# A fused mixture-of-experts layer on one core: the first loads dealt to two queues, and new ranks for the order of the work

## The chip, the cores and the metric

The kernel runs on one core of a Trainium2 chip. A core has a matrix engine (TensorE, PE in the profile, with its weight loads as PEld), three engines for everything else (VectorE, DVE; ScalarE, ACT; GpSimd, POOL) and SyncE (SP), which here only issues transfers. Transfers between the chip's main memory and the core's memory are carried by 16 DMA engines; an instruction on SP, ACT or POOL issues one. Each engine works through its own list of instructions in order and waits on semaphores for the others. The metric is the time of one execution in microseconds (us), as the median of several runs.

## The reference

Sixteen sequences of 256 tokens with 256 features go through a layer of eight experts and one shared expert. Every token goes through every expert, and the outputs are weighted for each sequence:

```python
E, B, S, D, F = (8, 2, 256, 256, 1024)   # B is 16 in the call
h = hidden_states
g = jnp.einsum('bsd,edf->ebsf', h, Wg)
u = jnp.einsum('bsd,edf->ebsf', h, Wu)
expert_outs = jnp.einsum('ebsf,efd->ebsd', jax.nn.silu(g) * u, Wd)
expert_output = jnp.einsum('be,ebsd->bsd', gating_probs, expert_outs)
shared = jnp.einsum('bsf,fd->bsd', jax.nn.silu(h @ Sg) * (h @ Su), Sd)
sg = shared_gate_prob[:, :, None]
return x + (1.0 - sg) * expert_output + sg * shared
```

All values are 32-bit floats. Wg, Wu and Wd are the weights of gate, up and down.

## The kernel before

The work is cut into 72 units, `units` in line 1361: nine experts, two halves of the 1024 hidden features, four groups of four sequences, the group innermost. A unit multiplies the tokens of its group by half an expert's gate and up weights, applies silu and the product, and multiplies by half of the down weights. To save matmuls, four token blocks and four weight blocks are combined (sums and differences in pairs) so that fewer products give all the blocks; this is why there are so many additions on VectorE and GpSimd. PE products carry the names D (the four diagonal pairs), M and X (the six pairs off the diagonal) and dn (the down product). Units 4 to 55 keep sums over experts in another form (`star`, line 640), units 56 to 71 go back to the first form. Unit 0 is plain: it multiplies the raw tokens by the raw weights (lines 814 to 853), since it comes first and the combined forms are not there yet.

Nothing is issued in the order in which it is written. Each piece of work is an `Op` with an engine, an estimated length, a rank, and what it depends on; `load` (line 358), `tt` and `stt` (lines 364 to 374) and `mm` (line 644) make them. `Plan.run` (line 105) then plays through the program once while it is being built: whenever an engine comes free, it takes from what is ready there the piece of the lowest rank. PE's pieces go strictly by rank, in two streams (the up side and dn). What comes out is a fixed list for each engine. The table `RANK` (line 25) holds the numbers that ranks are made of; many of them apply only to some units. `seed`, `sc`, `p` and `st` belong to the units of the star form, `wq` and `wqa` to the units from 56 on, `ph`, `hX`, `hA`, `hD`, `hE`, `hF` and `hG` to the sums of tokens and weights that units 1 to 4 make, `hR` to the sums of group 0's raw tokens, `pa` to a scaling on ScalarE in the pairs of weights (`make_pair`, line 416), `back` to the moments at which buffers return after the star form.

The start runs like this. `make_raw` (line 546) loads the four token blocks of group 0 (256 KB each, called x0 to x3 below, tile `side`), PE transposes each (line 561), ScalarE copies the result to `pq` (line 566). `load_base` (line 383) loads a half of the gate or up weights in two loads of 256 KB, for features 0 to 127 (`u`) and 128 to 255 (`v`), into a tile `wb`; sums are later made in the second part, so `load_raw` (line 443) loads features 128 to 255 of gate and up once more, into a tile of its own. Unit 0 reads `u` of `load_base` as its first half and the tile of `load_raw` as its second. The lines that set the order are these:

```python
        if n == 0:
            make_raw(0, (-14, -6.97), (-20, -18.6))
            load_base(0, e, half, -16, (-19, -16))
            first_raw = load_raw((-18.8, -17.5))
            load_base(1, e, half, -15, (-18, -15))
            make_raw(1, (-5.5, -5.5), (-17, -17))
```

The last pair of each line is the ranks of its loads. On SP the order that follows is: x0; gate's first half; gate's second half (called G2 below); x1; up's first half; up's second half; x2; x3; then gate's and up's `v`; then the tokens of groups 1 and 2. Before all of that GpSimd issues two broadcasts of the routing weights, `p_bc` and `coef` (lines 335 and 339), and PE runs nine products of zeros (line 354) while it has nothing else. The first two columns of gate's product are taken in halves (lines 827 to 843), so that x0 can be used before x1 is there.

Of the kernel before, what the change touches and what calls it, by code (L numbers as in the profile page):

```python
# [22 lines left out]


RANK = {
    "first": 4, "q": 2.85, "dc": 2.45, "acc": 2.55, "g": -5.35, "cp": 1.85, "seed": -0.3, "s": 0.75,
    "lagx": 1.0, "sc": 15.85, "bank": (6.6, 7.1, 8.6, 15.9, 16.4, 16.9, 17.3), "ev": 0.3, "p": 2.3,
    "xc": 0.2, "st": 1.2, "qa": -2.0, "da": -1.25, "ga": -7.25, "pace": 2, "m0": 1.9, "m1": 2.5, "xm":
    0, "w": 16, "mp": 4, "m2": 1.5, "ml": 1.75, "lagw": 1.0, "wp": -0.95, "wq": -0.9, "wqa": -2.25,
    "wdc": 2.2, "ws": 0.5, "wseed": 0.2, "wxc": 0.95, "pa": -4.25, "hd": (), "ph": 7.25, "pd": 1.0,  # L30
    "xh": 5, "hX": 4.5, "hA": 10.5, "hR": 5.0, "hD": -6.5, "hE": 5, "hF": -7.75, "hG": -3.75, "to":
    (-18, -3, -9, -16, -46), "back": (-27, 120, 21, -15, -5, 80, 20),
}


# [29 lines left out]
class Plan:  # L65
# [27 lines left out]
    def add(self, engine, length, rank, emit, deps=(), new=(), uses=(), lag=None, kb=None, port=False):  # L93
        lag = self.HOP if lag is None else lag
        op = Op(engine, length, lag, rank, emit, deps, list(new), list(uses))
        for b in [*op.new, *op.uses]:
            b.users += 1
        op.kb = kb
        op.port = port
        if engine == "PE" and op.new and op.new[0].tag == "dn" or "dn" in [b.tag for b in op.uses]:  # L100
            op.stream = 1 if engine == "PE" else None
        self.ops.append(op)
        return op
# [101 lines left out]
def kernel(  # L205
# [112 lines left out]
    def act(n):  # L318
        return 0.21 + n * 0.000625
# [38 lines left out]
    def load(rank, dst, src, kb, deps=(), new=(), uses=(), late=0, engine="SP"):  # L358
        queue = {"SP": nc.sync, "ACT": nc.scalar}[engine]
        return add(  # L360
            engine, 0.5, rank, lambda: queue.dma_start(dst(), src), deps, new, uses, lag=2.2 + late, kb=kb  # L361
        )

    def tt(engine, rank, o, a, b, op, n, deps, new=(), uses=(), port=True):
        eng, length = (nc.vector, dve(n)) if engine == "DVE" else (nc.gpsimd, pool(n))
        return add(engine, length, rank, lambda: eng.tensor_tensor(o(), a(), b(), op), deps, new, uses, port=port)  # L366
# [9 lines left out]
    def sources(e):  # L376
        return (Wg[e], Wu[e], Wd[e]) if e < E else (Sg, Su, Sd)
# [5 lines left out]
    def load_base(m, e, half, rank, ranks=None):  # L383
        b = Buf("wb", f"wb_{m}_{e}_{half}")
        src = [
            sources(e)[m][ts(part, P), ts(half, 4 * P)].rearrange("p (c q) -> p c q", q=P)
            for part in range(2)
        ] if m < 2 else None
        late = 0 if rank < 0 else 8
        ru, rv = ranks or (rank, rank)  # L390
        if m == 2:
            rows = sources(e)[2][ts(half, 4 * P), :].rearrange("(c p) (k q) -> p c k q", p=P, q=P)
        if m == 2:
            u = v = load(ru, lambda: b.tile, rows, 512, [], [b], late=late)
        else:
            u = load(ru, lambda: b[:, :, 0, :], src[0], 256, [], [b], late=late)
            v = load(rv, lambda: b[:, :, 1, :], src[1], 256, [], [], [b], late=late)
        ops = []
        for i, t in enumerate(POINTS):
            r, x_ = (lambda i=i: b[:, i, 1, :]), (lambda i=i: b[:, i, 0, :])  # L400
            if t == 0:
                op = v
            elif abs(t) == 1:
                op = tt("POOL", rank + 1, r, r, x_, ALU.add if t > 0 else ALU.subtract, P, [u, v], uses=[b])
            elif e == half == 0:
                op = stt(rank + 1, r, x_, float(t), r, ALU.add, P, [u, v], uses=[b])
            else:
                twice = Buf("wp", f"twice_{m}_{e}_{half}")
                op = add(
                    "ACT", act(P), rank + 1, lambda: nc.scalar.mul(twice[:, 0, :], x_(), float(t)), [u, v], [twice], [b]  # L410
                )
                op = tt("POOL", rank + 1, r, r, lambda: twice[:, 0, :], ALU.add, P, [op], [], [b, twice])
            ops.append(op)
        base[m, e, half], baseop[m, e, half] = b, (u, ops)
# [28 lines left out]
    def load_raw(ranks):  # L443

        b = Buf("wb", "wb_raw")
        ops = [
            load(
                ranks[m], lambda m=m: b[:, :, m, :],
                sources(0)[m][ts(1, P), 0 : 4 * P].rearrange("p (c q) -> p c q", q=P), 256,
                [], [b] if m == 0 else [], [b] if m else [],  # L450
            )
            for m in range(2)
        ]
        return b, ops
# [183 lines left out]
    FIRST, LAST = RANK["first"], NE * NHALF * NG - RANK["w"]  # L638
# [724 lines left out]
    for n, unit in enumerate(units):  # L1363
        e, half, g = unit
        r0 = W * n
# [6 lines that stand above are left out]
        elif g == 0:  # L1372
            for m in range(2):
                load_base(m, e, half, r0 - W + 3 * m - 8)
        if g == 0:
            for k in range(len(PAIRS)):
                for m in range(2):
                    make_pair(m, e, half, k, r0 + 2 * k + m - (RANK["ph"] if n == 4 else 8 if n else -4))
            if not star(n):
                load_down(e, half, r0 + W - 8)  # L1380
            else:
                load_base(2, e, half, r0 - 3)
                for k in range(len(PAIRS)):
                    make_pair(2, e, half, k, r0 + 2 * k + (RANK["pd"] if n == 4 else 1))
        if n == end:
            rows = load_rows(e, half, r0 - 2)
        if n == 1:
            for a in range(2):
                make_xd(g, a, -3.4 + 2 * a, -14, RANK["hD"] + 2 * a)
            for k in range(len(PAIRS)):  # L1390
                make_xp(g, k, RANK["hX"] + k)
            for a in range(2):
                make_xd(2, a, 3.2 + 2 * a, -13, RANK["hE"] + 2 * a)
            for k in range(len(PAIRS)):
                make_xp(2, k, RANK["hA"] + k / 2, True)
        elif n == 3:
            for a in range(2):
                make_xd(g, a, r0 - W + 6 * a - 4, r0 - W + 6 * a - 6, r0 - W + 6 * a + RANK["hF"])
            for k in range(len(PAIRS)):
                make_xp(g, k, r0 + 2 * k + RANK["hG"])  # L1400
        elif n == 4:
            for a in range(2):
                load_xd(g, a, r0 - W + 6 * a - 4)
            for k in range(len(PAIRS)):
                make_xp(g, k, r0 + 2 * k - RANK["xh"])
        elif n:
            if n > 2:
                for a in range(2):
                    load_xd(g, a, r0 - W + 6 * a - 4)
            for k in range(len(PAIRS)):  # L1410
                load_xp(g, k, r0 + 2 * k - 5)
        if n == end:
            basis = finish(g, load_pieces(g, IN_W, r0 - 2 * W + 1), r0 - 2 * W + 4, r0 - 2 * W + 10.3, False)
        if star(n):
            unit_down(n, unit, *unit_up(n, unit))
            continue
        for k in range(NG):
            if n == LAST + min(11 + k, int(RANK["m0"] + RANK["m1"] * k + RANK["m2"])):
                merge(k, W * (LAST + RANK["m0"] + RANK["m1"] * k))
        hb, hops = unit_up_w(n, unit)  # L1420
        if n == end:
            last_down(n, unit, hb, hops, rows, basis)
        elif n == end - 1:
            pieces = load_pieces(g, IN_EV, r0 + W - 1)
            unit_down_w(n, unit, hb, hops, pieces)
            finish(g, pieces, r0 + 2 * W + 1, r0 + 2 * W + 4.2)
        elif n > end - NG:
            unit_down_w(n, unit, hb, hops)
            finish(g, load_pieces(g, IN_W, r0 + 2 * W + 2), r0 + 2 * W + (4, 11)[g], r0 + 2 * W + (11, 13.5)[g])
        else:  # L1430
            unit_down_w(n, unit, hb, hops)
# [73 lines left out]
```

## Time and profile before

| | us |
|---|---|
| median of 3 runs (2485.01 to 2485.07) | 2485.02 |
| the profiled execution | 2482.88 |
| its span, first to last instruction | 2480.8 |
| PE busy | 2469.3 |
| PE busy in the first 20.00 of the span | 14.92 |
| PE busy from 20 to 40, from 40 to 60 | 20.00, 19.76 |
| PE busy in the last 41 (2440 on) | 36.67 |

The profile is of one execution, and its span leaves out a little at both ends. Engines are busy while their own instructions run; issuing a transfer is not counted. A row of the timeline gives start and length in us, engine, line, operation, the tiles written and read, how many instructions of the kind stand together, and in brackets the idle time of the engine before it, with what ended it. In a list of transfers the last number is the time from issue to landing. Lines of the profile name helpers: 647 is any matmul, 361 any load, 366 and 371 the additions.

### The profile page before, as it was taken

To read this page: it belongs to the slowest core of one execution; us is meant where nothing else is said; L and a number is where in the kernel's file an instruction comes from. 1 tells how busy PE (TensorE), PEld (TensorE's weight loads), DVE (VectorE), ACT (ScalarE), POOL (GpSimd) and SP (SyncE) were. 2 spreads that over 40 slices of the span, in tenths; PEclk is the share of its full clock that TensorE was granted. 3 is DMA by queue.
4 is the path that set the end of the run, shared out by engine and by line. 5 is a ranking of instruction groups with operands and counts; after the bars stand their busy time and mean duration, and the time that the engine had idled before them with its cause. 6 is when DMAs were issued, how large, how long until landed. Compare 5 with 4: busy or idle time off the path is not lost.

```text
span 2480.8 us, 35084 instructions
## 1 busy us (share of the span) xinstructions
PE 2469.3 (100%) x10894; PEld 2055.7 (83%) x10894; DVE 1857.2 (75%) x3142; ACT 1606.0 (65%) x3373; POOL 1807.2 (73%) x1947
## 2 busy tenths in 40 slices
PE   9999999999999999999999999999999999999999
PEld 5778888888888888888888888888888777777777
DVE  6787777777777777777767777777777788888787
ACT  3357777777787777777777777777777333333331
POOL 6886777768585868677776858586766687877874
PEclk9999999999999999999999999999999999999999
DMA  7545688888898888898888898888888877887666
GB/s 254 184 159 213 211 218 222 209 216 211 222 218 220 207 206 216 213 221 215 216 204 223 210 223 213 208 211 207 220 213 226 235 202 202 217 223 208 172 191 208
DMA packets 195769, 525.08 MB, mean 212 GB/s; under 512 B 16864, under 2 KB 83440, under 8 KB 186112
## 3 DMA queue, kind: packets, MB, share of 16 engines
q0 software_dynamic: 39552, 214.52, 45.1%
q1 hardware_dynamic: 156032, 308.33, 36.2%
q8 instruction: 87, 1.43, 0.2%
q14 instruction: 98, 0.80, 0.1%
HBM read 290.53 MB, written 232.26 MB: 211 GB/s over the span
## 4 chain that ended last, share of the span: by engine, by line
PE 99%; ACT 1%; DMA 0%; DVE 0%; issue 0%; SPq 0%; DVEq 0%
PE dn L647 33%; PE X L647 25%; PE M L647 20%; PE D L647 20%; DMA wb<-in_L_cond_Wg_dram 0%; PE dn L1311 0%; ACT sg L894 0%; PE dn L522 0%; ACT sg L885 0%; PE dn L561 0%; ACT wp L438 0%; SPq L361 0%; DVE X L366 0%; DVEq L1500 0%; ACT pq L674 0%
## 5 line engine op out<-in xcount | busy, mean ns | idle before, releaser
L366 POOL TENSOR_TENSOR s<-pq,pq 128x512 f32<-128x512 f32 x852 | 1116.0, 1337 | 450.0 <-DVE X L366 347.1
L366 DVE TENSOR_TENSOR X<-M,s 128x512 f32<-128x512 f32 x697 | 466.8, 692 | 155.7 <-PE M L647 98.9
L647 PE MATMUL X<-xp,wp 128*128 128x256 f32 x2204 | 570.2, 379 | 0.0
L647 PEld LDWEIGHTS X<-xp,wp 128*128 128x128 f32 x2204 | 418.4, 190 | 82.8 <-issue 24.6
L647 PE MATMUL D<-xd,wb 128*128 128x256 f32 x1760 | 454.6, 380 | 1.4 <-ACT sg L894 0.8
L647 PE MATMUL M<-xp,wp 128*128 128x256 f32 x1732 | 448.3, 379 | 0.3 <-DVE X L366 0.3
L647 PEld LDWEIGHTS D<-xd,wb 128*128 128x128 f32 x1760 | 333.2, 190 | 74.5 <-issue 22.9
L885 ACT ACTIVATE sg<-sg,coef 128x256 f32<-128x256 f32 x832 | 393.1, 510 | 2.4
L647 PEld LDWEIGHTS M<-xp,wp 128*128 128x128 f32 x1732 | 328.8, 190 | 70.6 <-issue 23.2
L1123 ACT COPY ev<-dn 128x512 f32<-128x512 f32 x451 | 261.7, 587 | 137.7 <-PE dn L647 134.7
L366 DVE TENSOR_TENSOR pq<-D,pq 128x256 f32<-128x256 f32 x568 | 229.9, 416 | 107.6 <-PE D L647 101.0
L921 DVE TENSOR_TENSOR big<-big,X 128x1024 f32<-128x1024 f32 x233 | 281.6, 1209 | 0.0
L647 PE MATMUL dn<-h,wp 128*128 128x256 f32 x1040 | 271.6, 379 | 0.5 <-ACT ev L1123 0.4
L366 DVE TENSOR_TENSOR X<-X,sg 128x512 f32<-128x512 f32 x233 | 162.0, 695 | 110.9 <-ACT sg L885 68.9
L674 ACT COPY pq<-D 128x512 f32<-128x512 f32 x284 | 167.2, 589 | 114.4 <-PE D L647 108.0
L647 PEld LDWEIGHTS dn<-h,wp 128*128 128x128 f32 x1040 | 197.2, 190 | 29.4 <-POOL wp L366 0.8
L894 ACT ACTIVATE sg<-X 128x512 f32<-128x512 f32 x236 | 142.0, 602 | 109.0 <-PE X L647 107.4
L647 PE MATMUL dn<-h,low 128*128 128x512 f32 (+1 forms) x498 | 199.0, 503 | 0.0
L1046 ACT COPY ev<-dn 128x512 f32<-128x512 f32 x123 | 72.0, 586 | 163.9 <-PE dn L647 162.7
L1123 ACT COPY big<-dn 128x512 f32<-128x512 f32 x225 | 130.8, 587 | 69.2 <-PE dn L647 67.3
L366 DVE TENSOR_TENSOR low<-X,h 128x256 f32<-128x256 f32 x233 | 97.5, 419 | 94.2 <-ACT h L969 93.8
L647 PE MATMUL M<-xp,low 128*128 128x256 f32 x592 | 157.5, 379 | 0.0
(161 smaller groups left out, 3911.2 us busy)
## 6 DMA issues: line engine op xcount, KB each, us to landing
xp<-keep_p SPq DMA_DIRECT2D x408, 384.0 KB, 5.0
star<-ev POOLq DMA_DIRECT2D x105, 768.0 KB, 6.9
xd<-keep_d SPq DMA_DIRECT2D x136, 512.0 KB, 3.6
star<-big POOLq DMA_DIRECT2D x51, 768.0 KB, 7.0
star<-ev POOLq DMA_DIRECT2D x34, 1024.0 KB, 11.9
total<-ev POOLq DMA_DIRECT2D x18, 1024.0 KB, 7.9
star<-big POOLq DMA_DIRECT2D x18, 1024.0 KB, 11.3
total<-ev POOLq DMA_DIRECT2D x17, 768.0 KB, 6.9
```

The costliest lines, as they stand in the source:

```text
L366: return add(engine, length, rank, lambda: eng.tensor_tensor(o(), a(), b(), op), deps, new, uses, port=port)
L647: lambda: nc.tensor.matmul(o(), w(), mv(), start=start, stop=stop, skip_group_check=onto),
L674: lambda: nc.scalar.copy(p_[:, 2 - 2 * a : 4 - 2 * a, :], bank[:, :, :]), ps,
L885: lambda: nc.scalar.mul(b[:, h, :], b[:, h, :], coef[:, e, 4 * g + block : 4 * g + block + 1]),
L894: lambda: nc.scalar.activation(b[:, :, :], bank[:, :, :], AF.Silu), deps, [b], [bank],
L921: "DVE", dve(4 * TB), rank, lambda: nc.vector.tensor_tensor(view(), view(), twice(), ALU.add),
L1046: lambda ev=ev, at=at, bank=bank: nc.scalar.copy(ev[:, at, :], bank.tile.rearrange("p a t -> p (a t)")),
L1123: lambda ev=ev, at=at, bank=bank: nc.scalar.copy(ev[:, at, :], bank.tile.rearrange("p a t -> p (a t)")),
```

## The change

Two things are changed. `load` already has an argument for the issuing engine; now the first half of gate's weights in `load_base` and gate's part in `load_raw` pass ACT, so that these two loads are issued by ScalarE. All other loads stay on SP. And fifteen entries of `RANK` are others, as are three of the seven numbers of `back`. A third edit, in the moment at which `merge` is called, only writes 11 as `RANK["w"] - 5` and gives the same number, since `w` is 16.

```diff
-    "first": 4, "q": 2.85, "dc": 2.45, "acc": 2.55, "g": -5.35, "cp": 1.85, "seed": -0.3, "s": 0.75,
-    "lagx": 1.0, "sc": 15.85, "bank": (6.6, 7.1, 8.6, 15.9, 16.4, 16.9, 17.3), "ev": 0.3, "p": 2.3,
-    "xc": 0.2, "st": 1.2, "qa": -2.0, "da": -1.25, "ga": -7.25, "pace": 2, "m0": 1.9, "m1": 2.5, "xm":
-    0, "w": 16, "mp": 4, "m2": 1.5, "ml": 1.75, "lagw": 1.0, "wp": -0.95, "wq": -0.9, "wqa": -2.25,
-    "wdc": 2.2, "ws": 0.5, "wseed": 0.2, "wxc": 0.95, "pa": -4.25, "hd": (), "ph": 7.25, "pd": 1.0,
-    "xh": 5, "hX": 4.5, "hA": 10.5, "hR": 5.0, "hD": -6.5, "hE": 5, "hF": -7.75, "hG": -3.75, "to":
-    (-18, -3, -9, -16, -46), "back": (-27, 120, 21, -15, -5, 80, 20),
+    "first": 4, "q": 2.85, "dc": 2.45, "acc": 2.55, "g": -5.35, "cp": 1.85, "seed": -0.8, "s": 0.75,
+    "lagx": 1.0, "sc": 14.35, "bank": (6.6, 7.1, 8.6, 15.9, 16.4, 16.9, 17.3), "ev": 0.3, "p": 2.05,
+    "xc": 0.2, "st": 0.95, "qa": -2.0, "da": -1.25, "ga": -7.25, "pace": 2, "m0": 1.9, "m1": 2.5, "xm":
+    0, "w": 16, "mp": 4, "m2": 1.5, "ml": 1.75, "lagw": 1.0, "wp": -0.95, "wq": -0.4, "wqa": -2.5,
+    "wdc": 2.2, "ws": 0.5, "wseed": 0.2, "wxc": 0.95, "pa": -3.5, "hd": (), "ph": 7.0, "pd": 1.0, "xh":
+    5, "hX": 7.25, "hA": 9.75, "hR": 2.5, "hD": -11.25, "hE": 8.5, "hF": -8.75, "hG": -4.25, "to": (-18,
+    -3, -9, -16, -46), "back": (-27, 117, 15, -15, -11, 80, 20),
@@
-            u = load(ru, lambda: b[:, :, 0, :], src[0], 256, [], [b], late=late)
+            u = load(ru, lambda: b[:, :, 0, :], src[0], 256, [], [b], late=late, engine="ACT" if ranks and m == 0 else "SP")
@@
-                [], [b] if m == 0 else [], [b] if m else [],
+                [], [b] if m == 0 else [], [b] if m else [], engine=("ACT", "SP")[m],
@@
-            if n == LAST + min(11 + k, int(RANK["m0"] + RANK["m1"] * k + RANK["m2"])):
+            if n == LAST + min(RANK["w"] - 5 + k, int(RANK["m0"] + RANK["m1"] * k + RANK["m2"])):
```

The changed program, built but not run, has these loads in this order: on ACT gate's first half ahead of everything, then the table load and the small activation of line 329, then G2; on SP x0, x1, up's first half, up's second half, x2, x3, and the rest as before. On PE the transposes of x1 now stand ahead of the first product that reads G2.

## The prediction

> **What bounds the kernel now.** I read the page first, then the waits of the matrix engine (PE), then the first 16 us as a timeline, then the transfers of that stretch.
>
> ```profile
> span 2480.8 us, 35084 instructions
> PE 2469.3 (100%) x10894; PEld 2055.7 (83%) x10894; DVE 1857.2 (75%) x3142; ACT 1606.0 (65%) x3373; POOL 1807.2 (73%) x1947
> ```
>
> PE is busy for all but 11.5 us of the span. It keeps one pace: in the trace a 256-column matmul starts 216 ns after the last one, a 512-column one 429 ns, a 128-column transpose 109 ns. Start to start, everything above that pace adds up to 10.7 us: 4.68 us before 12.2 us, 6.0 us in small pieces from 45 us on. Before the first matmul lie 1.2 us, behind the start of the last one 4.5 us. So a change of loads and order can gain little; 0.2% of 2485.02 us is 4.97 us, about what a measurement of this kernel can tell from no change.
>
> ```profile
> PE X L647 <- DMA wb<-in_L_cond_Wg_dram: 3.0, 1, 3.0
> PE X L354 <- DVE zero L327: 1.2, 1, 1.2
> PE X L647 <- ACT pq L566: 0.9, 2, 0.7
> PE D L647 <- ACT sg L894: 0.8, 2, 0.4
> ```
>
> One wait is long, 3.0 us, and it is for a load that the change touches. Its place:
>
> ```profile
> 1.23 1.01 SPq L361 DMA_DIRECT2D wb<-in_L_cond_Wg_dram  x2
> 2.28 0.51 SPq L361 DMA_DIRECT2D side<-in_x_dram  x1
> 5.25 0.59 ACT L566 COPY pq<-dn 128x512 f32<-128x512 f32 x1 [3.01 <-PE dn L561]
> 9.55 1.13 PE L647 MATMUL X<-pq,wb 128*128 128x256 f32 x4 [2.97 <-DMA wb<-in_L_cond_Wg_dram]
> 10.52 0.60 PE L561 MATMUL dn<-ident,side 128*128 128x128 f32 x4
> 10.96 0.60 PE L647 MATMUL X<-pq,wb 128*128 128x256 f32 x2
> 11.16 0.59 ACT L566 COPY pq<-dn 128x512 f32<-128x512 f32 x1 [5.32 <-PE dn L561]
> 11.79 1.99 PE L647 MATMUL X<-pq,wb 128*128 128x256 f32 x8 [0.24 <-ACT pq L566]
> 13.62 1.88 PE L647 MATMUL M<-pq,wb 128*128 128x512 f32 x4
> ```
>
> PE waits until 9.55 for the second half of gate's weights (the second of the two wb loads at 1.23, issued 1.74), works 0.97 us, transposes the second token tile, and waits 0.40 us more for its copy. From 13.62 to 45 us it never waits. Why does a load issued at 1.74 land at 9.5?
>
> ```profile
> GB/s 0 0 22 297 311 157 178 111 59 173 326 346 356 315 309 307 292 279 328 351 356 321 343 348 354 334 301 295 326 324 310 310 284 354 408 406 423 416 423 385
> p_bc<-in_fside_Bx_dram POOLq DMA_DIRECT2D x1, 64.0 KB, 5.4
> coef<-ondB_sharedgateprob_dram POOLq DMA_DIRECT2D x1, 8.0 KB, 6.6
> ```
>
> Slices are 0.75 us. The rate falls from 311 to 59 GB/s between 3.75 and 6.75 us, while the two broadcasts that GpSimd issued (p_bc, coef) are under way; their packets hold an engine for up to 1.7 us each, the last until about 8.5 us. [...] The landings: first tokens x0 3.69, gate's first half 5.11, second half G2 9.51, x1 10.29, up's halves 11.17 and 11.99, x2 12.75, x3 13.46; one every 0.7 to 0.9 us after the hole. That is the engines' pace, not that of the issues (0.43 to 0.51 us each at first; the later ones take 1.2 to 2.0 [...]).
>
> **The change, part by part.**
>
> *Two queues.* SyncE (SP) loses two issues, so x1 goes from 2.28 to about 1.2 us and the rest move up. ScalarE (ACT) gains two. Gate's first half goes ahead of its table load (1.28 us at 0.74), which then ends near 2.5; the 0.20 us activation behind it ends near 2.7; only then is G2 issued, about 1.0 us later than now. Two issues at 0.43 to 0.51 us end near 3.2, and ACT's first work, the copy at 5.25, has 3.01 us of idle before it: cost nothing; without that cover 1 us. If ACT's queue filled as SP's does (up to 1.99 us an issue) the copy would be late, but PE would still be waiting for G2. G2's later issue is hidden as well: today it still lies unserved 3 us after its issue.
>
> What counts is G2's landing, W. The trace has no load of this kernel on ACT's queue, so I bound it. By the row alone: ACT's queue holds nothing before G2 but gate's first half, so it lands as now, 9.51, or ahead of the hole, near 6. The Trainium skill speaks against that ("DMA: Bandwidth & Descriptors", section "Issuing engines are not separate DMA queues": loads from several engines run on the same 16 engines and interleave, and only issue time is saved; section "Queues, rings and completion order": an engine takes the queues in turn, packet by packet). No row here shows SP's and ACT's queues at work at once. By the rule x0 shares with gate's first half and x1 with G2, four loads of 256 KB that are down at 10.29 today. On the engine that is slowest today the first 512 KB are through before the hole in either order; the other 512 KB run together after it, so x1 and G2 land at about 9.7 to 10.5 both. I take W = 10.3, since every landing after the hole is bound by the same engines; ends 6 and 10.9 (up's first half creeping in behind x1).
>
> *PE's order.* In the changed program x1's transposes stand ahead of the first use of G2. PE then starts at W + 0.04, runs six matmul instructions (6 x 0.216 = 1.30, 0.10 for the restart) while ACT copies x1, and eight more (1.73): the up matmuls, now at 13.62, start at W + 3.17. Today it is 9.51 + 4.11. So the new order is worth 0.94 us: transposes 0.44 and copy wait 0.40 off the path, and one restart of 0.10. At W = 10.3 they start at 13.47: gain 0.15 us. At 9.51 the gain is 0.94. Break-even is W = 10.45. The order adds a wait: if x1 lands after W - 0.48, everything waits for it (x1 + 0.04 + 0.44 + 3.13); at x1 = 10.29 that is 13.90, a loss of 0.28. Earlier W is capped: group 1's second tokens land at 16.43 (the twelfth load of 256 KB in either order) and are transposed at 18.37, so at most 1.9 us can be kept.
>
> *Ranks.* They only reorder instructions. Set side by side, the two programs have the same order on every engine from about 70 us on, apart from one VectorE (DVE) step near 1960 us, moved three places back; the many changes in ranks of the later units change nothing there. So the small stalls from 128 us on (0.28 at 128, 0.60 at 183, a dozen up to 0.65 from 1230 on) stay. Of the moves before 70 us:
> - DVE: a difference of group 2 (0.42 to 0.95 us in the rows of this line) and a multiplication (0.39 to the next start) go ahead of the step that frees a dn bank, now 35.64 to 36.04; a dn matmul at 36.91 uses that bank, with 0.87 us of slack. Put back by 0.8 to 1.3: 0 to 0.5 us lost, 0.1 taken, by the shorter rows, which are the common ones.
> - Group 1's last two pair sums and their stores go back from 31 to 34 us to about 42 to 50. PE uses them at 73.68 and 78.85: nothing. SP's stores behind them wait with them; the loads of up's next weights, now issued at 49.47 and down at 54.11, go behind one more store (52.46): up to 3 us later, first read by ACT at 61.42: nothing.
> - PE: half a dn product goes ahead of the D pair at 59.01 and another from 60.74 back to about 64. The D pair's distance to its second pass falls by 1.72 of 2.23 us slack: 0.5 left, nothing.
> - ACT: a 0.30 us scaling from 58.88 goes ahead of the copy at 53.10, into 1.09 us of idle: nothing.
> - POOL waits for a moved sum at about 52 with two s tiles behind it; they start some 2 and 4 us later than now (51.95 and 55.04), needed at 59.04 and 64.35 by DVE: nothing, 0.5 us if the covers are short.
> - The stall of 0.51 at 53.74 comes from PE's own order, which is unchanged there.
>
> *Sum.* Against the profiled execution (2482.88 us, span 2480.8 and 2.1 around it): start -0.15 by the shared rule, ranks +0.1. With W between 9.5 and 10.6 the start gives -0.94 to +0.15, and the ranks' ends are 0 and +0.5, so the case's band is -0.9 to +0.5 or so. Since the new order's 0.94 is certain work taken off the path and only W's shift eats it, I take -0.5, not the -0.05 of W = 10.3 alone: span 2480.3, time 2482.4. The median of three runs is 2.14 us above the profiled one, and I move it by the same: 2485.02 - 0.5 = 2484.5 us.
>
> **Rivals.**
> - *Shared landing (likeliest, 0.52).* As summed: 2484.1 to 2485.5. For it: the landings of before follow the engines' pace.
> - *G2 comes early (0.35).* ACT's queue gets its turn on every engine before the broadcasts hold it, or the broadcasts get a smaller share. Gain 0.9 to 1.9, plus up to 0.3 where later stalls shrink: 2482.8 to 2484.1. For it: nothing but gate's first half is ahead of it. Against it: on the slowest engine today nothing of G2 moved between 5 and 8.5 us.
> - *G2 starves (slower, 0.09; of these 0.03 by over 0.2%).* G2, issued 1 us later, shares each engine with x1 and up's halves and lands last of the six, at 12: 12 + 3.17 = 15.17, a loss of 1.55, 2486.6. It decides from W = 10.45 on; for 4.97 us W would have to be 15.5, later than all eight first loads today.
> - *A new stall behind the ranks (slower, within the 0.09 beside it, 0.02).* Only if a store in the new order holds DVE's buffer.
> - *More than 4.97 us faster (0.02).* That needs the whole start (at most 3.4 of 4.68) and the stalls to 183 us (1.66) together.
> - *No effect at all* lies inside the first case.
>
> **How the numbers follow.** 0.52 and 0.35 and most of the slower cases lie within 0.2%. Over 0.2% faster 0.02, slower 0.04, the rest 0.94. The range takes the first two cases and the slower one as far as W = 11.7: 2482.8 to 2486.2; the likeliest alone is 2484.1 to 2485.5.
>
> **What would show it.** Right: p_bc's hole still there, x1 and G2 landing within 0.8 us of each other near 10, x1's transposes ahead of the 9.55 wait, up's first matmul within 0.4 us of 13.62, the same stalls at 128, 183 and 1366 us. Wrong: G2 landing before 9.5, a hole that is shorter, or PE waiting between 20 and 80 us where it does not now.

## The result

| | before | after |
|---|---|---|
| median of 21 executions each, taken side by side, us | 2484.31 | 2480.26 |
| lowest and highest, us | 2481.35 to 2485.82 | 2479.83 to 2482.0 |
| ratio, 95% interval | | 0.9986 (0.998 to 0.9991) |
| the profiled execution, us | 2482.88 | 2480.25 |
| its span, us | 2480.8 | 2478.4 |

The change makes the kernel 4.05 us (0.14%) faster. That is a gain that the interval separates from nothing, but one below the 0.2% of the forecast's classes. The forecast, 2484.5 with a range from 2482.8 to 2486.2, missed it: the gain was larger than its cases of any weight allowed.

The page's first lines, after:

```profile
span 2478.4 us, 35075 instructions
PE 2469.9 (100%) x10894; PEld 2056.2 (83%) x10894; DVE 1856.5 (75%) x3142; ACT 1605.8 (65%) x3373; POOL 1808.5 (73%) x1947
```

PE's waits, after. The wait of 3.0 us for gate's weights is gone, and no wait of PE is for a transfer. One wait is new, the last line shown (dots stand for lines left out):

```profile
PE X L354 <- DVE zero L327: 1.2, 1, 1.2
PE D L647 <- ACT sg L894: 0.8, 2, 0.4
PE X L647 <- ACT pq L566: 0.7, 1, 0.7
...
PE D L647 <- ACT sg L789: 0.3, 1, 0.3
...
```

The start as a timeline, after:

```profile
0.74 0.50 ACTq L361 DMA_DIRECT2D wb<-in_L_cond_Wg_dram  x1
1.28 1.28 ACT L329 ACT_TABLE_LOAD   x1 [1.28 <-PEq L1491]
1.31 0.74 POOL L335 DMA_DIRECT2D p_bc<-in_fside_Bx_dram  x1 [0.36 <-issue]
1.34 0.46 ACTq L361 DMA_DIRECT2D wb<-in_L_cond_Wg_dram  x1
...
5.01 1.06 PE L561 MATMUL dn<-ident,side 128*128 128x128 f32 x4
6.75 0.70 PE L647 MATMUL X<-pq,wb 128*128 128x256 f32 x2 [0.67 <-ACT pq L566]
7.29 0.60 PE L561 MATMUL dn<-ident,side 128*128 128x128 f32 x4
7.72 3.19 PE L647 MATMUL X<-pq,wb 128*128 128x256 f32 x14
10.75 1.88 PE L647 MATMUL M<-pq,wb 128*128 128x512 f32 x4
```

G2 (the second load on ACT's queue) is issued at 1.34, while the table load runs until 2.56. It is down 5.2 us later, at 6.55, before PE begins its first product of the tokens at 6.75. The up matmuls start at 10.75 instead of 13.62. The rate in slices of 0.75 us, and the two broadcasts:

```profile
GB/s 0 0 31 173 275 323 347 318 131 264 92 77 350 386 352 295 300 330 348 348 348 350 350 348 337 307 292 319 345 321 293 300 341 399 433 378 418 414 404 421
p_bc<-in_fside_Bx_dram POOLq DMA_DIRECT2D x1, 64.0 KB, 5.6
coef<-ondB_sharedgateprob_dram POOLq DMA_DIRECT2D x1, 8.0 KB, 7.3
```

The hole is still there, and about as wide. It has moved from 3.75 to 6.75 us to 6 to 9 us, behind the loads that PE waits for first. Landings: x0 4.17, gate's first half 4.83, x1 5.76, G2 6.55, up's halves 7.98 and 10.04, x2 10.79, x3 11.57.

How the 4.05 us are made up: the two profiled executions differ by 2.63, and the median of before lies 1.43 above its profile while that of after lies 0.01 above its own. Matmul by matmul, after is 2.88 us ahead at the up matmuls and stays so until 40 us; at 41.33 it loses 0.52; from there to the end it stays 2.36 ahead. So three things want explaining: why G2 came 3 us earlier, what stalls at 41 us, and why most executions of before are slower than its profile.

### The profile page after: what moved, and what is told of

The parts are those of the page before. It is cut to its first block, busy times and chain, and to the rows that moved or that the text cites. A ratio compares the mean times of both kernels' runs of the same rounds, so it can differ in the third digit from the quotient of the medians.

```text
span 2478.4 us, 35075 instructions
## 1 busy us (share of the span) xinstructions
PE 2469.9 (100%) x10894; PEld 2056.2 (83%) x10894; DVE 1856.5 (75%) x3142; ACT 1605.8 (65%) x3373; POOL 1808.5 (73%) x1947
## 3 DMA queue, kind: packets, MB, share of 16 engines
q8 instruction: 87, 1.43, 0.2%
## 4 chain that ended last, share of the span: by engine, by line
PE 99%; ACT 1%; DVE 0%; issue 0%; DVEq 0%; ACTq 0%
PE dn L647 33%; PE X L647 25%; PE M L647 20%; PE D L647 20%; PE dn L1311 0%; ACT sg L894 0%; PE dn L522 0%; PE X L354 0%; ACT sg L885 0%; PE dn L561 0%; ACT wp L438 0%; DVE pq L366 0%; DVE big L371 0%; DVE X L366 0%; ACT sg L789 0%
## 5 line engine op out<-in xcount | busy, mean ns | idle before, releaser
L647 PE MATMUL dn<-h,low 128*128 128x512 f32 (+1 forms) x486 | 193.9, 501 | 0.0
```

The costliest lines, as they stand in the source:

```text
L647: lambda: nc.tensor.matmul(o(), w(), mv(), start=start, stop=stop, skip_group_check=onto),
```

## The experiments

Each of them ran with before beside it on the same chip; "below before" is the difference of these two medians. How far such a difference can be trusted is shown by before itself: run once more (again, below), it came out 0.52 us under the before beside it. Theory and rivals stand in the expectations.

### One part of the change at a time

```diff
# queues: after, with before's ranks
-    "first": 4, ... "seed": -0.8, ... "hX": 7.25, "hA": 9.75, ...
+    "first": 4, ... "seed": -0.3, ... "hX": 4.5, "hA": 10.5, ...
# ranks: before, with after's ranks
-    "first": 4, ... "seed": -0.3, ... "hX": 4.5, "hA": 10.5, ...
+    "first": 4, ... "seed": -0.8, ... "hX": 7.25, "hA": 9.75, ...
```

> The two queues alone, with before's ranks. Theory (turns: the loads and the broadcasts take turns on the transfer engines, and a second queue puts two more loads ahead of the broadcasts' turn): G2 down at 6.3 to 7.0 us as with the whole change, up matmuls at 10.7 to 11.5 instead of 13.6, no stall of 0.5 us near 41 us; span about 2.5 to 3.0 us below before's, median 3.5 to 5 below. Rival (the ranks bring it): G2 early, but the median less than 1.5 us below.

> The new ranks alone, with one queue. Theory (turns): G2 down at 9.3 to 9.8 us, a wait of about 3 us for it as before, up matmuls at 13.0 to 13.6 (0.3 to 0.9 us of gain if x1's transposes stand ahead), the stall of 0.5 us near 41 us present: within 1 us of before. Rival (the ranks bring most of the 4 us): median 3 us or more below before.

| | median | before | ratio (interval) | G2 down | up matmuls | span |
|---|---|---|---|---|---|---|
| queues | 2480.80 | 2484.62 | 0.9986 (0.9978 to 0.9995) | 6.60 | 10.74 | 2479.1 |
| ranks | 2484.86 | 2484.62 | 1.0004 (0.9995 to 1.0013) | 9.38 | 15.27 | 2483.0 |

The queues bring the start, 3.82 us of median, and the ranks alone bring nothing that can be told from zero. Two things were not as expected. With the ranks alone the up matmuls started at 15.27 although G2 was on time: PE worked at half speed there, of which more below. And the queues alone had a stall that neither kernel has, near 26.4 us. Their timeline (copies and activations of ACT, and PE):

```profile
25.40 1.04 PE L522 MATMUL dn<-ident,h 128*128 128x128 f32 x8
26.04 0.37 ACT L527 COPY xd<-dn 128x256 f32<-128x256 f32 x1 [4.15 <-PE dn L522]
26.30 0.42 ACT L613 ACTIVATE xp<-xp 128x256 f32<-128x256 f32 x1
...
26.62 0.59 ACT L789 ACTIVATE sg<-D 128x512 f32<-128x512 f32 x1
...
27.26 0.48 PE L647 MATMUL D<-xd,wb 128*128 128x256 f32 x1 [0.83 <-ACT sg L789]
```

ACT has been idle for 4.15 us, yet its activation of D comes last: ahead of it in ACT's list stands the copy of a transpose that PE makes only at 25.40. `Plan.run` times the loads too, so another queue for two of them moves its whole order, and with before's ranks it puts that copy ahead of the activation, which it follows in both of the other kernels. At the end of the program this kernel is 1.72 us ahead of before's profile, the whole change 2.36. So by the two profiles the new ranks are worth some 0.6 us beside the queues. The medians do not show it: 4.05 below before with the ranks, 3.82 without, the same ratio of 0.9986. Without the queues the ranks bring nothing that can be told.

### What holds G2 back

First the broadcasts are taken out of the way on the old kernel, with its one queue and its order of work:

```diff
# late: before, both broadcasts behind an addition that reads G2's tile
-    nc.gpsimd.dma_start(p_bc..., probs...)
-    nc.gpsimd.dma_start(coef[:, E, :], ...)
+    def broadcasts():
+        first = first_raw[0].tile[:, 0, 0, :]   # part of G2
+        nc.gpsimd.tensor_tensor(held[:, :], first, first, ALU.add)
+        nc.gpsimd.dma_start(p_bc..., probs...)
+        nc.gpsimd.dma_start(coef[:, E, :], ...)
...
+    # called, with make_coef behind it, when the plan has emitted G2's load
```

> Before, with both broadcasts issued by GpSimd only after G2 has landed; one queue, old ranks. Theory (turns: G2 is late because two broadcasts stand ahead of it on the engines): G2 down at 5.5 to 6.2 us from the single queue, x1 at about 6.5, no wait of PE over 0.5 us, median 3 to 5 us below before: the second queue isn't needed. Rival (one queue can't bring the first loads faster, its issues are too far apart): G2 at 8 us or later, median within 1.5 us of before.

Measured: 2480.48, 4.14 below before (0.9984, 0.9975 to 0.9992). G2 is down at 5.89, x1 at 6.63, the up matmuls start at 10.81. G2's load in before, and then in late with PE's first up matmul (line numbers are shifted by 5):

```profile
wb<-in_L_cond_Wg_dram SPq DMA_DIRECT2D x1, 256.0 KB, 7.8
```

```profile
wb<-in_L_cond_Wg_dram SPq DMA_DIRECT2D x1, 256.0 KB, 4.2
...
10.81 1.88 PE L652 MATMUL M<-pq,wb 128*128 128x512 f32 x4
```

So one queue brings the first loads as fast as two do; what cost 3 us was the broadcasts ahead of G2. What puts them there, the number of queues or the moment of issue? Four kernels shift one or the other:

```diff
# delay: before
+    nc.gpsimd.memset(held, 0.0)
+    for _ in range(3):
+        nc.gpsimd.tensor_tensor(held, held, held, ALU.add)
     nc.gpsimd.dma_start(p_bc..., probs...)
# delay2: before; written into p_bc and coef themselves, which the broadcasts overwrite
+    flat = p_bc.rearrange("p b e -> p (b e)")
+    nc.gpsimd.memset(flat, 0.0)
+    for _ in range(3):
+        nc.gpsimd.tensor_tensor(flat, flat, flat, ALU.add)
+    nc.gpsimd.tensor_tensor(coef[:, E, :], p_bc[:, :, 0], p_bc[:, :, 0], ALU.add)
     nc.gpsimd.dma_start(p_bc..., probs...)
# g2late, g2mid: after, in front of G2's load; three times in g2late, once in g2mid
+    nc.vector.memset(b[:, :, 0, :], 0.0)
     nc.scalar.dma_start(b[:, :, 0, :], ...)
+    # and make_coef, which reads the broadcasts on VectorE, placed behind G2's load
```

> Before, with four small GpSimd operations ahead of or between the two broadcasts, so that p_bc is issued about 1.0 us later (2.3 instead of 1.31) and coef at about 3.7; one queue, old ranks. Theory A (first come, first served: what counts is which was issued first): G2, issued at 1.74, is ahead of p_bc and lands at 5.5 to 6.2, the gain is 3 us or more as with the broadcasts held back altogether. Theory B (turns between queues: with one hardware queue the broadcasts get their turn behind the second load whatever is queued ahead of them): G2 lands later than 7.5 us and the median is within 1.5 us of before.

> Before, with five small GpSimd operations ahead of both broadcasts, so that p_bc is issued at 2.4 to 3.0 us and coef after it; one queue, old ranks. Theory A (order of issue: a broadcast goes behind the loads that were issued before it, coef jumps one or two of them): G2, issued at 1.74, and x1, issued at 2.28, are ahead of p_bc: G2 at 5.5 to 6.3, x1 at 6.3 to 7.2, no wait of PE over 1 us, median 3 to 4.5 us below before. Theory B (turns: one load behind the other for each 0.4 us is chance): G2 later than 7 us.

> The whole change, with G2 held back on ScalarE's queue: its tile is first written three times by VectorE, so that it is issued at 2.3 to 3.0 us instead of 1.34, which is what the prediction took for it or later. Theory A (first come, first served): p_bc, issued at 1.31, is now ahead of G2, which lands at 8 us or later; PE waits 1.5 us or more for it; median 1 to 3 us above the whole change. Theory B (turns between queues): G2 still gets the turn behind x1 and lands by 7.0; median within 0.5 us of the whole change.

> The whole change with one write to G2's tile ahead of its load, so that G2 is issued at about 1.8 us on ScalarE's queue, 0.5 later than in the change. Theory A (order of issue, over both hardware queues): it lands between 7.2 and 9.6, close to up's first half, which is issued at 1.74; the whole change's other loads stay where they are; median 0.7 to 3 us above the whole change. Theory B (a queue's turn doesn't depend on when it was filled): G2 within 0.5 us of 6.55.

Issues and landings in us, from the transfers in each trace:

| kernel | G2 issued, by | p_bc, coef issued | loads issued ahead of p_bc | p_bc, coef down | G2 down | median below before |
|---|---|---|---|---|---|---|
| before | 1.74, SP | 1.31, 2.37 | 2 | 6.70, 8.94 | 9.51 | |
| delay | 1.74, SP | 1.72, 2.80 | 2 | 7.11, 9.56 | 7.75 | 0.89 |
| delay2 | 1.74, SP | 3.33, 4.05 | 5 | 9.33, 11.47 | 6.33 | 3.95 |
| late | 1.74, SP | 6.31, 7.02 | 10 | 11.94, 13.27 | 5.89 | 4.14 |
| after | 1.34, ACT | 1.31, 2.37 | 3 | 6.91, 9.67 | 6.55 | 4.05 |
| g2mid | 1.71, ACT | 1.30, 2.36 | 3 | 6.91, 9.59 | 8.59 | 3.39 |
| g2late | 3.03, ACT | 1.30, 2.36 | 3 | 6.65, 8.94 | 11.65 | -2.29 |
| hA (further below) | 1.34, ACT | 1.30, 2.37 | 3 | 7.05, 9.51 | 7.55 | 4.53 |

(delay came out weaker than meant: one of its additions was placed between the broadcasts and one behind them, so that p_bc moved by 0.41 us only, still ahead of G2. Its numbers are those of its theory B, but with p_bc still issued first they do not speak against theory A; delay2, which does put G2's issue first, came out as A.)

What counts is when a load is issued, not on which queue. On the same two queues, 0.37 us in G2's issue are 2.04 us in its landing between after and g2mid, and 1.69 us are 5.10 between after and g2late. Of the 2.04 only half is sure: hA issues its first loads at after's times to 0.01 us, and its G2 landed at 7.55, 1.00 later than after's and behind p_bc, where after's came ahead of it. G2's issue and p_bc's are 0.03 to 0.04 us apart in these two, and either can land first; g2mid's G2 is 1.04 beyond the later of them. The single issues in lists of transfers, first of after, from 1.3 to 1.4 us, then of g2mid at 1.71:

```profile
wb<-in_L_cond_Wg_dram ACTq DMA_DIRECT2D x1, 256.0 KB, 5.2
```

```profile
wb<-in_L_cond_Wg_dram ACTq DMA_DIRECT2D x1, 256.0 KB, 6.9
```

And of g2late: G2's load, and what the queues moved (packets, MB, share of 16 engines) from 5 to 7.9 us and from 8 to 11 us; q10 is ACT's queue, q1 SP's, q0 GpSimd's.

```profile
wb<-in_L_cond_Wg_dram ACTq DMA_DIRECT2D x1, 256.0 KB, 8.6
...
q1 hardware_dynamic: 893, 0.45, 59.4%
q0 software_dynamic: 41, 0.04, 38.9%
...
q1 hardware_dynamic: 902, 0.70, 72.4%
q10 hardware_dynamic: 527, 0.26, 29.9%
q0 software_dynamic: 15, 0.00, 0.3%
```

G2 was issued at 3.03 and was alone in its queue, gate's first half being down at 5.04. From 5 to 7.9 us its queue does not appear at all, while SP's moves 0.45 MB; G2's first packet is at 8.36, and from then on both queues move. It landed among the loads that SP issued just before and after it: x2, issued at 2.80, at 10.83, x3, issued at 3.35, at 11.67. PE waited 4.5 us for it:

```profile
11.69 4.80 PE L657 MATMUL X<-pq,wb 128*128 128x256 f32 x14 [4.50 <-DMA wb<-in_L_cond_Wg_dram]
```

Its median lies 6.3 us higher against before than the change's, where theory A had expected 1 to 3: these 14 products also ran at half speed at first, as the next part shows.

In every one of these traces the first eight loads of 256 KB of SP and ACT landed in the order of their issue, whichever queue they were on (where two were issued within 0.03 us, in either order). The broadcasts fit in less strictly. p_bc comes behind about as many loads as had been issued before it, and coef overtakes one or two: it was down before x1 in delay though issued 0.52 us behind it. Why coef overtakes, and why G2 lands 0.9 us earlier in g2mid than in before when it was issued within 0.03 us of the same time, is open; the trace does not say which engine carried which packet.

### Why most executions of before are slower than its profile

```diff
# fill: before; two products behind x0's transposes, eight behind the first product of the tokens
+        for _ in range(pads.get(op, 0)):
+            nc.tensor.matmul(banks[2]..., zero[:, 0:P], zero, start=True, stop=True)
```

> Before, unchanged, for a second profile. Theory (the 3 us in which PE stands still at 6.6 to 9.6 lets the array's clock fall to half in some executions, which the first profile didn't catch): G2 at 9.3 to 9.8 again, and either a span of about 2480.8 or, with matmuls of 256 columns at 427 ns behind 9.6 us for up to 3.4 us, a span 1 to 1.7 us longer. Rival (the clock does not fall): the span is within 0.3 us of 2480.8 and matmuls stand 216 ns apart from 9.6 us on.

> Before with ten more products of zeros on PE, two behind x0's transposes and eight behind the first product of the raw tokens, where PE stands still for G2. Theory (a pause of PE lets the array fall to half speed, and that is what lifts most executions of before above its first profile): G2 still at about 9.5 us, but no matmuls at half speed behind it; up matmuls at 13.5 to 13.9; median 1.0 to 1.8 below before's, and a narrower spread. Rival (the spread of before has another cause): median within 0.3 of before's, spread as wide.

again (before once more): 2484.10, and its own profile, span 2482.0, shows what the first one did not. PE from 10.04 to 13.55 us and from there to 15 us; the columns are the stretch, its length, PE's busy time with the matmuls, the granted clock, the transfers' busy share, GB/s. First again, then before's first profile:

```profile
10.04:13.55 3.51, 3.51 (x11) 0.51 1.11 318
13.55:15.00 1.45, 1.45 (x8) 1.00 1.11 336
```

```profile
10.04:13.55 3.51, 3.27 (x17) 1.00 1.04 300
13.55:15.00 1.45, 1.45 (x6) 1.00 1.03 340
```

For 3.5 us the array ran at half its clock, and made 11 matmuls where it made 17 in the first profile. G2 had landed at the same time in both (9.46 and 9.51); the up matmuls start at 14.85 instead of 13.62, and the 1.22 us stay to the end. In the profile of ranks the array is at half speed from the start to 13.6 us (matmuls of 256 columns 427 ns apart); g2late reads 0.50 from 12.0 to 13.6.

fill only keeps PE at work in that pause:

```profile
7.48 1.89 PE L1466 MATMUL X<-zero 128*128 128x512 bf16 x8
9.21 1.06 PE L647 MATMUL X<-pq,wb 128*128 128x256 f32 x4
```

It takes 2482.55, 1.76 below before (0.9992, 0.9984 to 1.0001, which just takes in 1), with G2 down at 9.09 and the up matmuls at 13.21; some 0.4 us of the gain may be this earlier G2. Its eleven executions lie within 1.04 us, those of before beside it within 4.15. 3.5 us at half clock in 2482 us make a mean of 0.9993. 25 of the 33 executions of before that were run beside again show a mean granted clock of 0.998 or 0.999, and 31 of the 33 beside fill; all 11 of fill and all 21 of after show 1.0. (The record shows the clock's fall. Where it never rose, as in the profile of ranks up to 13.6 us, it reads 1.00, so 25 is a lower bound for before, and the 1.0 of fill and after says that the clock did not fall there, not that it always rose early.) The clock records and the narrower spread speak for the theory more plainly than the medians: PE's pause of 2 to 3 us ahead of 9.5 lets the clock fall in most executions, and before's first profile was one of the few without.

The Trainium skill describes such a clock ("TensorE: Matmul & The Clock Gate", section "Part 1: The HAM clock gate (the "warmup" mystery)"): a free-running window of 3413 ns, half speed behind an idle one, full speed behind a busy one, so that the same program meets it at another phase each time. The 3.51 us of half clock in again, the array's rise just behind 4.16 us in before and past 5.6 us in again, and the spread agree with it. One thing does not: the pause ahead of again's fall was 2.1 us, shorter than that window, so no wholly idle window was needed here.

### The stall at 41 us, and a better version

```diff
# hA: after
-    5, "hX": 7.25, "hA": 9.75, ...
+    5, "hX": 7.25, "hA": 10.5, ...
```

> The whole change with one rank, hA, put back from 9.75 to 10.5, which puts the 1.46 us VectorE step (ev) behind the two additions to pq instead of ahead of them. Theory (that step is what makes PE stand still for 0.42 us near 41.3): no wait for sg there, span 0.4 to 0.6 below the whole change, unless PE's order, which moves a little up to 70 us, loses some of it. Rival (another cause): the same stall near 41 us.

VectorE, ACT and PE in after, and then in hA:

```profile
38.07 1.46 DVE L371 SCALAR_TENSOR_TENSOR ev<-xd,ev 128x256 f32<-128x256 f32 x1
39.45 0.41 DVE L366 TENSOR_TENSOR pq<-D,pq 128x256 f32<-128x256 f32 x1
...
40.18 0.41 DVE L366 TENSOR_TENSOR pq<-D,pq 128x256 f32<-128x256 f32 x1
...
40.68 0.60 ACT L789 ACTIVATE sg<-D 128x512 f32<-128x512 f32 x1 [3.82 <-DVE pq L366]
...
41.33 0.92 PE L647 MATMUL D<-xd,wb 128*128 128x256 f32 x3 [0.26 <-ACT sg L789]
```

```profile
38.51 0.42 DVE L366 TENSOR_TENSOR pq<-D,pq 128x256 f32<-128x256 f32 x1 [1.22 <-PE D L647]
...
39.74 0.60 ACT L789 ACTIVATE sg<-D 128x512 f32<-128x512 f32 x1 [2.61 <-DVE pq L366]
...
40.88 1.03 PE L647 MATMUL D<-xd,wb 128*128 128x256 f32 x4
```

In after a sum of group 2 goes ahead of the two additions to pq and takes 1.46 us; the additions free D for ACT, and ACT for PE. With it out of the way the stall is gone, and the profile's span is 2478.0 instead of 2478.4. The median is 2479.78 (0.9982, 0.9974 to 0.9991), 4.53 below before against the change's 4.05. This points the same way, but the intervals of the two ratios overlap. (Why that sum takes 1.46 us, where a step of this form takes 0.42 in hA, was not tested. A POOL addition of 1.27 us runs beside it in after; in hA one as long runs beside VectorE steps of 0.41 to 0.47 us, on other operands.)

Two kernels then tried for the rest of the start:

```diff
# hAlate: hA with the broadcasts of late
# best: hAlate, and
-    for n in range(9):
+    for n in range(7):
         nc.tensor.matmul(..., zero[:, 0:P], zero, ...)
+    # two more behind x0's transposes
```

> The whole change with hA put back to 10.5 and both broadcasts held until G2 has landed. Theory A: all eight first loads come one behind the other, G2 at 5.6 to 6.3, x3 at 10.0 to 10.6; but PE is held by x0's transposes and copy, not by G2, so that only 0 to 0.4 us come off against the change with hA alone. Rival (the broadcasts still cost the start): 0.5 us or more off.

> The same with seven products of zeros ahead of x0's transposes instead of nine, and two behind them. Theory (with the loads out of the way PE's start is held by the nine zero products, which end at 5.0 while x0 is down at about 4.2): first product of the tokens at 5.7 to 6.1 instead of 6.75, up matmuls at 9.7 to 10.2, median 0.5 to 1.0 below the same kernel with nine. Rival (the shorter run of zero products leaves the array at half speed for longer): as much or more is lost to matmuls at 427 ns.

hAlate: 2479.95 (0.9984, 0.9975 to 0.9993), G2 at 6.82, later than expected and no earlier than in after. By the medians, then, the broadcasts cost the start of hA nothing that can be told. The profile cannot say more, since it caught one of two executions (2481.62 and 2481.64) that lie some 1.5 us above the other nine. The array came to full speed only at 10.3 us in it, though PE had no long pause and the clock's record reads 1.00; the 14 products that take 3.19 us in after took 4.10, and the up matmuls start at 12.54:

```profile
8.61 4.10 PE L652 MATMUL X<-pq,wb 128*128 128x256 f32 x14
12.54 1.88 PE L652 MATMUL M<-pq,wb 128*128 128x512 f32 x4
```

So a late rise of the clock can strike the kernels without the pause too; one of after's 21 executions, at 2482.0, may be such a one. best: 2479.93 (0.9982, 0.9973 to 0.999). Its first product of the tokens starts at 6.32 instead of 6.75, but at half speed (589 ns to the next), and the up matmuls at 10.71: the rival was right, the zero products pay for themselves in clock. Against the before beside each, hA, hAlate and best are 4.53, 4.54 and 4.56 us faster: nothing between them can be told. None of best's eleven executions is a late one as hAlate's two are, but eleven are too few to give the two added products the credit.

## Why the prediction was wrong, by its own steps

- **"G2 ... issued, about 1.0 us later than now" failed, and with it the frame of everything after.** The step took for granted that ACT's queue of work stands still behind the table load. It does not: G2 was issued at 1.34 during the load of 1.28 to 2.56 us, and ahead of the activation that stands before it in ACT's list (2.58), 0.40 earlier than before instead of 1.0 later. g2late is the forecast's premise made true (3.03 instead of about 2.7), and it runs as the rival "G2 starves" said: W = 11.65, a time of 2486.6 us, where the rival had 12 and 2486.6. That the times agree is in part luck, since the measured one has matmuls at half speed in it as well.
- **W = 10.3 "by the shared rule" failed**: measured 6.55. x1 and G2 do not run side by side behind the hole. The loads landed in the order of their issue, and the second queue counts only because four loads are issued by 1.34 us where there were two by then. That nothing of G2 moved on the slowest engine between 5 and 8.5 us was no row's: the trace does not say which engine carried which packet. Of the two sections of the Trainium skill, "Issuing engines are not separate DMA queues" in "DMA: Bandwidth & Descriptors" was the useful one after all, read the other way round: only issue time is saved, but that put x1's issue ahead of p_bc's and G2's within 0.03 us of it, and G2 lands 3 us earlier for it (2 us in hA). The turns by packet between queues, of its other section "Queues, rings and completion order", did not show in g2late from 5 to 7.9 us, where G2's queue got none; from 8.36 us on both queues moved.
- **The rival "G2 comes early" named the right landing and the wrong reason, so its landing was luck.** Its "ACT's queue gets its turn" is what g2mid and g2late refute: on the same queue, issued later, G2 did not get it. Its gain of 0.9 to 1.9 was too small.
- **"The up matmuls start at W + 3.17" held only while G2 is last.** Where it is last and the array at full speed the rule is exact: 8.59 gives 11.76 in g2mid and 7.55 gives 10.72 in hA, both as measured. At W = 6.55 it gives 9.72; measured 10.75. In after's profile x0 sets the start: zero products until 5.01, transposes and a first product at 6.75, and 14 products of 0.216 us from 7.72. That is 0.86 later than before's first product of the tokens (5.89), since the array was still at half speed there: x0's transposes stand 0.213 us apart, in before's profile 0.109. The order itself came out as told, x1's transposes ahead of G2.
- **The cap of 1.9 us failed.** It rested on "16.43 in either order" for the twelfth load; that one landed at 14.86. (It was issued at 8.01 instead of 11.18; whether this or the place of the hole brought it forward was not tested.) The start kept its 2.88 us.
- **Ranks: the size fell at the edge of the band by luck, the place was missed.** "0 to 0.5 us lost" stands against 0.52, but at 41.33, by a sum ahead of the additions to pq, and not at the dn product that the step had followed. The slack was reckoned with the durations of before (0.42 to 0.95 us for such a step); in its new place it took 1.46. "The stall of 0.51 at 53.74" stayed, 2.4 us earlier. What the step could not see, since it compared only the two programs, is that the ranks mend what the new queues do to the plan: without them the loss is 1.1 us by 43 us (the stall behind 26.4), not 0.5.
- **"The median of three runs is 2.14 us above the profiled one, and I move it by the same" failed.** It was no constant: 1.43 us of it (by 21 executions) went with PE's pause, and by the clock records it was for the most part the array's clock, lost in that pause: 1.22 in the one execution that again shows, up to 1.76 by fill's median.

In sum, against the forecast's 0.5 (which was itself picked between a sum of 0.05 and a gain of up to 0.9): the start 2.88 instead of 0.15 to 0.94, the ranks' loss 0.52 instead of 0.1, the median's own part 1.43 instead of 0; the 0.26 that these leave of the 4.05 lie mostly outside the span (2.63 by the profiled times, 2.4 by the spans). The largest miss is the start, and its root is the landing of G2.

## What to carry to other kernels

At a kernel's start, count which transfer is issued before which, over all queues, because here 0.4 us of issue was 1 to 2 us of landing when something slow was issued at the same time; a small broadcast that nobody needs yet belongs behind the loads that the first matmul waits for. A pause of the matrix engine of 2 to 3 us cost more than its length here, since the array came back at half speed in most executions, and a single profile can miss it: compare its time with the median before taking it for the kernel. Where a planner orders the work, a change that looks local shifts its whole list, so take the parts of a change alone before judging one by the other.

## What the hardware showed that I had not expected

- ACT issued a transfer 0.06 us after its table load of 1.28 us had begun, not behind it.
- A load on its own hardware queue, alone there from 5.04 us on, moved nothing for 5.3 us (issued 3.03, first packet 8.36) while loads of another queue, issued before it, were served.
- The same load of 256 KB, G2, took from 4.2 us (late) to 8.6 us (g2late) from issue to landing, by what had been issued before it. With the same issue times it took 5.2 us (after) and 6.2 us (hA).
- The array's half-speed spell behind a pause lasted 3.5 us and cost 1.22 us in one execution and nothing in another of the same program, with the same landing of G2.
